# Cross-attention and a mixture-of-experts layer on one core: a fourth joint product, and a new order of the work in a quad

## The chip, the core and the metric

The kernel runs on one core of one Trainium2 chip. The metric is the device time of one execution in microseconds (us), lower is better. A core has five engines that each work through their own list of instructions in order and meet through semaphores: TensorE (PE; its weight loads are shown apart as PEld), VectorE (DVE), ScalarE (ACT), GpSimd (POOL) and SyncE (SP), which here issues all DMAs.

## The reference

For 8 batches of 1024 rows of 1024 float32 numbers:

```
x = x + attention(layernorm(x), ctx, mask)          # 64 context rows a batch, softmax over them
h = layernorm(x)
base = h @ weight.T                                  # 1024 x 1024
probs = softmax(h @ router_w.T)                      # 8 experts; the two best, renormalized
expert_out = sum over experts (w_dense * (h @ lora_A.T)) @ lora_B.T * 2     # rank 16 each
x = x + base + expert_out
```

Everything is computed in float32.

## The kernel before, in words

The 8192 rows are 64 tiles of 128 rows; two tiles (r = 0, 1) form a *pair*, 32 pairs in all, four pairs to a batch. The kernel is software-pipelined over pairs, and the main loop `quad(u)` handles the dense layer of pairs u and v = u+1 while it does the attention and the normalization of later pairs: n = u+2, m = u+3 and f = u+4. The order of instructions on TensorE, VectorE, ScalarE and SyncE is that in which the Python code calls them (a manual schedule), so the order of calls in `quad` is the order on each engine's queue. There are 15 quads (u = 2, 4, ..., 30); `start` and `first_joint` do pairs 0 and 1 and lead in.

**Dense layer.** The base product of a pair is done with seven block products instead of eight (a Strassen-Winograd scheme over two halves of rows, of depth and of columns). Products 1, 6, 7 and the low-rank term 8 of one pair follow each other in one PSUM bank, `chain`; after each, VectorE adds the bank to a quarter of x (`product_add`), and only then may the next product go on in the bank. Product 5 has a bank of its own (`b5`) and is added to two quarters. Products 2, 3 and 4 of two pairs are done *jointly* (`joint`): the same scheme once more, seven blocks of 256 columns instead of eight, in two banks. The sums that they need are made on VectorE (`rt_sums` of a pair, `joint_sums` of two pairs; `quarter_sums` of the weights, once).

**Low rank and router.** `rt_low_rank` multiplies a pair by 136 columns (128 low-rank and 8 router); ScalarE copies the result (`axl`), `rt_top` finds the two best experts on VectorE with one Exp on ScalarE and scales the low-rank numbers; `rt_turn_low_rank` transposes them on TensorE (`trw`), ScalarE copies that (`axwt`), and `lora` adds them to a bank.

**Attention of a pair.** `att_turn` transposes its rows on VectorE from a blocked load (`load_xs`, eight DMAs); `att_scores` (`sct`) multiplies them with the turned context memory (`memT`), ScalarE copies them, `att_sc` transposes them, `att_exp` and `att_divide` do the softmax with row statistics of x, `att_turn_p` transposes the probabilities (`ptp`), ScalarE copies them (`pt`), `att_readout` (`ro`) multiplies them with the memory into four banks, and `att_add` adds these to x. `x_stats` makes the row statistics on ScalarE (two passes with accumulation, then a square root).

**Normalization of a pair.** `norm_stats` makes means and variances on VectorE, `norm` applies them on ScalarE (h), writes h to DRAM and reads it back blocked (`norm_send`), and `rt_turn` transposes it on VectorE into hA and hB.

**Memory of a batch.** Once in four pairs `mask_bias`, `send_mem` (statistics and centring on VectorE, a round trip through DRAM, a scaling pass on ScalarE) and `turn_mem` prepare the next batch's context.

**What sets the order around the change.** Six PSUM banks serve all products, readouts and joints (`bank_of`), one bank the attention scores and probabilities, one the low rank. Six SBUF buffers (`ring`) serve blocked loads, turned rows, h and its reload. Five buffers hold x of pairs, so a load of x for m takes the buffer of pair u-2 and waits until that pair's rows are stored. SyncE issues its DMAs in order, and a DMA waits until the one eight places before it has landed.

Of the kernel before, what the change touches and what calls it, by code (L numbers as in the profile page):

```python
# [24 lines left out]
def kernel(  # L25
# [42 lines left out]
    small = ctx.enter_context(tc.tile_pool(name="small", bufs=2))  # L68
# [118 lines left out]
    def x_stats(u: int):  # L187

        sm = small.tile([P, 2, 1], F32, tag="sm", name=f"sm_{u}")
        nm = small.tile([P, 2, 1], F32, tag="nm", name=f"nm_{u}")  # L190
        ss = small.tile([P, 2, 1], F32, tag="ss", name=f"ss_{u}")
        for r in range(2):
            nc.scalar.activation(  # L193
                junk, xts[u][:, r, :], AF.Identity, accum_out=sm[:, r, :]
            )
        nc.scalar.mul(nm, sm, -1.0 / D)
        for r in range(2):
            nc.scalar.activation(  # L198
                junk, xts[u][:, r, :], AF.Square, bias=nm[:, r, :], accum_out=ss[:, r, :]
            )  # L200
        stds[u] = small.tile([P, 2, 1], F32, tag="std_att", name=f"std_att{u}")
        nc.scalar.activation(stds[u], ss, AF.Sqrt, bias=eps_sb[:, 1:2])

    xmv = {}

    def x_stats_vector(u: int, r: int):
        if r == 0:
            xmv[u] = small.tile([P, 2, 2], F32, tag="mv_att", name=f"mv_att{u}")
# [9 lines left out]
    junk = const.tile([P, D], mybir.dt.bfloat16, name="junk")  # L218

# [7 lines left out]
    def centre_mem(b: int, chunks: bool):  # L227
# [5 lines left out]
        if (b, "mv") not in mcs:  # L233
            mv = small.tile([P, 2], F32, tag="mv_mem", name=f"mv_mem_{b}")
# [16 lines left out]
    def turn_mem_pe(b: int, chunks: bool):  # L251
        mc = centre_mem(b, chunks)
        mt = memp.tile([P, KD, M], F32, tag="memT", name=f"memT_{b}_{chunks}")
# [17 lines left out]
    def turn_mem(b: int):  # L271
        mt = memp.tile([P, KD, M], F32, tag="memT", name=f"memT_{b}_True")
# [27 lines left out]
    def att_scores(u: int):  # L300
# [9 lines left out]
        scs[u] = small.tile([2 * M, P], F32, tag="tp", name=f"scts_{u}")  # L310
# [35 lines left out]
    def att_turn_p(u: int):  # L346
        ptp = ps_at.tile([2 * M, P], F32, tag="at", name=f"ptp_{u}")
        nc.tensor.transpose(ptp, ps.pop(u).rearrange("p j m -> p (j m)"), ident)
        pts[u] = small.tile([2 * M, P], F32, tag="tp", name=f"pt_{u}")
# [64 lines left out]
    has, hbs, axls, axwts, sms = {}, {}, {}, {}, {}  # L414
# [21 lines left out]
    def rt_low_rank(u: int):  # L436

        axls[u] = small.tile([P, 2, ER + E], F32, tag="axl", name=f"axl_{u}", bufs=1)
        pa = ps_rt.tile([P, 2, ER + E], F32, tag="rt", name=f"pa_{u}")
        for r in range(2):  # L440
            for k in range(KD):
                h = (has[u] if k < KH else hbs[u])[:, r, k % KH, :]
                mm(pa[:, r, :], h, art_sb[:, k, :], start=(k == 0), stop=(k == KD - 1))  # L443
        nc.scalar.copy(axls[u], pa)
# [32 lines left out]
    def rt_turn_low_rank(u: int):  # L477
# [4 lines left out]
        axwts[u] = small.tile([ER, 2, P], F32, tag="axwt", name=f"axwt_{u}")  # L482
# [16 lines left out]
    def rt_sums(u: int):  # L499

        outs = [
            sums.tile([P, KH, P], F32, tag=f"s{i}", name=f"s{i}_{u}", bufs=1 if i < 4 else 2)
            for i in range(1, 5)
        ]
        ha, hb = has[u], hbs[u]
        for do in block_sums(outs, ha[:, 0], hb[:, 0], ha[:, 1], hb[:, 1]):
            do()
        sms[u] = outs
# [37 lines left out]
    def block(bank, a, w, start: bool, between=None, after: int = 0):  # L546
        n = a.shape[1]
        for k in range(n):
            mm(bank, a[:, k, :], w[:, k, :], start=(start and k == 0), stop=(k == n - 1),  # L549
               skip_group_check=True)  # L550
            if k == after and between:
                between()
# [3 lines left out]
    def product(u: int, i: int, between=None, after: int = 0):  # L556

        if i == 1:
            pps[u] = bank_of(f"b5_{u}"), bank_of(f"ch_{u}")
# [3 lines left out]
        elif i == 5:  # L563
            block(b5, sms[u][0], t1, True, between, after)
        elif i == 6:
            block(chain, sms[u][1], t2, False, between, after)
        elif i == 7:
            block(chain, sms[u][2], t3, False, between, after)
# [11 lines left out]
    L2 = {2: (0, 0), 3: (0, 1), 4: (1, 0)}  # L580

    def joint_plain(i: int, p: int, between=None, after: int = 0):
# [4 lines left out]
            2: (hbs[p][:, 0], w21), 3: (sms[p][3], w22), 4: (hbs[p][:, 1], t4)  # L587
# [7 lines left out]
    def joint_sums(i: int, u: int):  # L595

        both = i != 3
        outs = [
            sums.tile([P, 2, HK, P], F32, tag=f"q{j}", name=f"q{j}_{i}_{u}")
            for j in range(1, 5)  # L600
        ]
        if both:
            up, lo = hbs[u], hbs[u + 1]
            do = block_sums(
# [378 lines left out]
```

## Time and profile before

| what | value |
|---|---|
| median of 3 runs | 1159.88 us (1159.77 to 1162.51) |
| profiled execution | 1160.02 us, its span 1158.2 us |
| mean granted TensorE clock | 0.995 |
| busy TensorE / VectorE / ScalarE | 1136.2 / 880.7 / 416.4 us |
| one quad in the middle | 69.25 us, or 69.58 us where the memory of a batch is prepared |
| DMA | 175.70 MB, 53.5% of 16 engines' span |

In lines of the profile, L549 is line 549 of the kernel. A group gives line, engine, operation, output tile <- input tiles, sizes and count, then busy time, mean ns of one instruction, and idle time before it with what ended it. A float32 product appears as two records on TensorE. In timelines the first number is the start from the span's beginning and the second the length, both in us; neighbours on TensorE overlap in their drain, so the distance from one start to the next is what a piece of work costs its queue. Where an instruction waited, the wait stands in brackets with its releaser.

### The profile page before, as it was taken

What the parts mean: (1) busy time and instruction counts of PE and PEld (TensorE: products, weight loads), DVE (VectorE), ACT (ScalarE), POOL (GpSimd) and SP (SyncE); (2) the same over time, 40 slices, a digit from 0 to 9 for tenths busy, and PEclk for the clock granted to TensorE, in tenths of its full rate; (3) what the DMA queues carried; (4) which work ended last, traced back from release to release, by engine and by line L of the source; (5) the groups of instructions that cost most, each with busy time, mean ns of one, the idle gap of its engine ahead of it and who ended that gap; (6) DMA issues with size and microseconds to landing.
All of it is one profiled execution on the core that took longest, in us unless ns stands there. A gap on an engine that the chain in (4) does not pass through costs nothing.

```text
span 1158.2 us, 15206 instructions
## 1 busy us (share of the span) xinstructions
PE 1136.2 (98%) x5314; PEld 741.9 (64%) x5314; DVE 880.7 (76%) x2216; ACT 416.4 (36%) x808; POOL 1.0 (0%) x16
## 2 busy tenths in 40 slices
PE   7899999999999999999999999999999999999998
PEld 6455567585665857567585765857567585765746
DVE  5867877887778787787787877788777887777754
ACT  4254333433235342333423234342333433234100
POOL 0000000000000000000000000000000000000000
PEclk8999999999999999999999999999999999999999
DMA  9437655464584635766355674445656374572401
GB/s 238 111 91 200 182 146 189 120 162 148 145 236 116 196 96 146 211 162 204 90 146 162 164 218 117 175 124 165 185 145 202 97 183 137 146 218 73 146 1 72
DMA packets 103549, 175.70 MB, mean 152 GB/s; under 512 B 11376, under 2 KB 75760, under 8 KB 103472
## 3 DMA queue, kind: packets, MB, share of 16 engines
q1 hardware_dynamic: 103472, 174.73, 53.5%
q8 instruction: 41, 0.67, 0.3%
q14 instruction: 36, 0.29, 0.1%
HBM read 107.84 MB, written 66.85 MB: 151 GB/s over the span
## 4 chain that ended last, share of the span: by engine, by line
PE 91%; DVE 5%; DMA 3%; issue 1%; SPq 0%; DVEq 0%
PE ch L549 28%; PE jl L549 13%; PE pa L443 10%; PE ju L549 9%; PE b L549 9%; PE ro L359 5%; PE sct L306 5%; PE jl L543 3%; PE ju L543 3%; PE ch L543 2%; PE j L549 2%; DMA w<-in_w_t_dram 2%; DVE xt L540 1%; DMA xs<-in_x_dram 1%; PE trw L481 1%
## 5 line engine op out<-in xcount | busy, mean ns | idle before, releaser
L549 PE MATMUL ch<-t,s 128*128 128x512 f32 x512 | 242.2, 600 | 3.8 <-DVE xt L540 3.6
L540 DVE TENSOR_TENSOR xt<-ch,xt 128x512 f32<-128x512 f32 x128 | 87.0, 679 | 94.4 <-PE ch L549 57.8
L549 PEld LDWEIGHTS ch<-t,s 128*128 128x128 f32 x512 | 89.8, 190 | 98.1 <-issue 86.9
L382 ACT ACTIVATE std_ffn<-mv_ffn,eps_sb 128x1 f32<-128x1 f32 x64 | 18.9, 296 | 281.0 <-DVE mv_ffn L183 265.9
L549 PE MATMUL ch<-w,hA 128*128 128x512 f32 x256 | 118.3, 605 | 0.1
L549 PE MATMUL b<-w,s 128*128 128x512 f32 x256 | 118.4, 592 | 0.0
L549 PEld LDWEIGHTS ch<-w,hA 128*128 128x128 f32 x256 | 48.0, 192 | 59.6 <-issue 58.4
L630 DVE TENSOR_TENSOR xt<-jl,xt 128x256 f32<-128x256 f32 x135 | 55.5, 411 | 37.3 <-PE jl L549 37.3
L540 DVE TENSOR_TENSOR xt<-ro,xt 128x512 f32<-128x512 f32 x128 | 79.2, 675 | 3.7 <-PE ro L359 3.7
L549 PEld LDWEIGHTS b<-w,s 128*128 128x128 f32 x256 | 46.4, 190 | 55.4 <-issue 54.9
L182 DVE BATCH_NORM_STATS2 st_ffn<-xt 128x6 f32<-128x512 f32 x128 | 80.5, 671 | 0.0
L400 ACT ACTIVATE h<-xt,nmr,rstd_ffn 128x1024 f32<-128x1024 f32 x60 | 71.1, 1232 | 12.3 <-DVE rstd_ffn L389 6.3
L443 PEld LDWEIGHTS pa<-art_sb,hA 128*128 128x128 f32 x512 | 66.3, 190 | 8.4 <-issue 7.4
L89 DVE STREAM_TRANSPOSE xT<-xs 128x1024 f32<-128x1024 f32 x60 | 70.8, 1218 | 0.0
L443 PE MATMUL pa<-art_sb,hA 128*128 128x136 f32 x512 | 69.8, 279 | 0.0
L443 PE MATMUL pa<-art_sb,hB 128*128 128x136 f32 x512 | 69.7, 279 | 0.0
L198 ACT ACTIVATE junk<-xt,nm 128x1024 bf16<-128x1024 f32 x60 | 69.0, 1151 | 2.0
L359 PE MATMUL ro<-mem,pt 64*128 64x512 f32 x256 | 65.4, 630 | 0.4 <-ACT pt L350 0.4
L443 PEld LDWEIGHTS pa<-art_sb,hB 128*128 128x128 f32 x512 | 64.1, 190 | 0.0
L193 ACT ACTIVATE junk<-xt 128x1024 bf16<-128x1024 f32 x60 | 63.6, 1059 | 0.9
L306 PEld LDWEIGHTS sct<-xT,memT_True 128*64 128x64 f32 x960 | 51.8, 137 | 16.6 <-DVE xt L540 10.6
L540 DVE TENSOR_TENSOR xt<-jl,xt 128x512 f32<-128x512 f32 x45 | 31.0, 689 | 41.3 <-PE jl L543 41.3
(151 smaller groups left out, 1767.6 us busy)
## 6 DMA issues: line engine op xcount, KB each, us to landing
out_dram<-xt SPq DMA_DIRECT2D x64, 512.0 KB, 4.4
xs<-in_x_dram SPq DMA_DIRECT2D x240, 128.0 KB, 4.9
xt<-in_x_dram SPq DMA_DIRECT2D x30, 1024.0 KB, 6.7
hd<-h SPq DMA_DIRECT2D x60, 512.0 KB, 2.8
hs<-hd SPq DMA_DIRECT2D x240, 128.0 KB, 3.3
mem<-in_ctx_dram SPq DMA_DIRECT2D x16, 256.0 KB, 6.8
w<-in_w_t_dram SPq DMA_DIRECT2D x16, 256.0 KB, 9.9
xt<-in_x_dram SPq DMA_DIRECT2D x4, 512.0 KB, 6.0
```

The costliest lines, as they stand in the source:

```text
L89: nc.vector.transpose(dst.rearrange("p k (t i) -> p t k i", i=NB), src.rearrange("p t (k i) -> p t k i", i=NB),)
L182: nc.vector.bn_stats(st[:parts, c, :], src[:, ts(c, HB)])
L193: nc.scalar.activation(junk, xts[u][:, r, :], AF.Identity, accum_out=sm[:, r, :])
L198: nc.scalar.activation(junk, xts[u][:, r, :], AF.Square, bias=nm[:, r, :], accum_out=ss[:, r, :])
L306: mm(sct[r * M : (r + 1) * M, :], mt[:, k, :], x_ts[u][r][:, k, :], start=(k == 0), stop=(k == KD - 1),)
L359: mm(ro, pts[u][rows, :], m[rows, ts(c, HB)], start=True, stop=True)
L400: nc.scalar.activation(h, xts[u][:, r, :], AF.Identity, bias=nmr, scale=rstd)
L443: mm(pa[:, r, :], h, art_sb[:, k, :], start=(k == 0), stop=(k == KD - 1))
L540: tt(xc, bank, xc, ALU.add)
L543: mm(bank, axwts[u][:, r, :], lb_sb[:, c0 : c0 + n], start=False, stop=True, skip_group_check=True)
L549: mm(bank, a[:, k, :], w[:, k, :], start=(start and k == 0), stop=(k == n - 1), skip_group_check=True)
L630: tt(xc, src, xc, ALU.add)
```

## The change

- **Product 5** is done jointly for two pairs from quad 2 on, by the function `joint`, with quarters of the weight block t1; it adds no low-rank term, and each add goes to both row tiles of x (the bank read twice, through a broadcast). `rt_sums` keeps its first and fourth sum side by side, so that one `joint_sums` serves products 5 and 3.
- **Joint products** 5, 3, 2, 4 follow each other. Other work is put between their seven blocks by numbered hooks.
- **Readout of a pair** stands right before the scores of the following pair: n before m, m before f. The attention of a pair is half a quad further ahead than before.
- **Low rank** of a pair is split by row tile and stands between products 1, 6 and 7 of the same pair.
- **Statistics** of the normalization go from VectorE to ScalarE (`f_sums`, `f_squares`, `f_std`, `f_rows`); those of the attention are split in three calls.
- **Loads**: the blocked rows of pair u+5 are loaded after the row-0 stores and ahead of the row-1 stores.
- The pool of small tiles has one buffer by default, with two for tiles that are named so.

```diff
-    small = ctx.enter_context(tc.tile_pool(name="small", bufs=2))
+    small = ctx.enter_context(tc.tile_pool(name="small", bufs=1))
...
+    def x_sums(u: int):
...
+        for r in range(2):
+            nc.scalar.activation(
+                nowhere, xts[u][:, r, :], AF.Identity, accum_out=sm[:, r, :]
+            )
+        nc.scalar.mul(nm, sm, -1.0 / D)
+        stds[u] = nm
...
+    def f_std(u: int):
+        nm, ss = fts[u]
+        std = small.tile([P, 2, 1], F32, tag="stdf", name=f"stdf_{u}")
+        nc.scalar.activation(std, ss, AF.Sqrt, bias=eps_sb[:, 0:1], scale=1.0 / D)
+        fts[u] = nm, std
+
+    def f_rows(u: int):
+
+        nm, std = fts.pop(u)
+        rstd = small.tile([P, 2, 1], F32, tag="rstdf", name=f"rstdf_{u}")
+        nc.vector.reciprocal(rstd, std)
+        nmr = small.tile([P, 2, 1], F32, tag="nmrf", name=f"nmrf_{u}")
+        tt(nmr, nm, rstd, ALU.mult)
+        for r in range(2):
+            h = ring.tile([P, D], F32, tag="ring", name=f"h_{u}_{r}")
+            hss.setdefault(u, []).append(h)
+            nc.scalar.activation(
+                h, xts[u][:, r, :], AF.Identity, bias=nmr[:, r, :], scale=rstd[:, r, :]
+            )
+        norm_send(u)
...
+    def rt_low_rank_tile(u: int, r: int):
+        if r == 0:
+            pas[u] = ps_rt.tile([P, 2, ER + E], F32, tag="rt", name=f"pa_{u}")
+        pa = pas[u]
+        for k in range(KD):
+            h = (has[u] if k < KH else hbs[u])[:, r, k % KH, :]
+            mm(pa[:, r, :], h, art_sb[:, k, :], start=(k == 0), stop=(k == KD - 1))
+        if r == 1:
+            axls[u] = small.tile([P, 2, ER + E], F32, tag="axl", name=f"axl_{u}", bufs=1)
+            nc.scalar.copy(axls[u], pas.pop(u))
...
-    def joint(i: int, u: int, early=(), fill=()):
+    def joint(i: int, u: int, hooks):
...
         block(p4, d[:, HK:], q4, True)
-        lora(v, p4, r, c * HB, HH)
-        for do in early[:1]:
-            do()
+        low(v, p4, 0)
+        hook(1)
         block(chain, a[:, :HK], b11, True)
         part(u, 0, chain)
-        for do in early[1:]:
-            do()
+        hook(2)
         block(p2, a[:, HK:], b21, True)
-        lora(u, p2, r, c * HB, HH)
+        low(u, p2, 0)
+        hook(3)
         block(p5, s1, q1, True)
         part(v, 1, p5)
+        hook(4)
         block(chain, s2, q2, False)
         part(u, 1, chain)
-        for do in fill:
-            do()
+        hook(5)
         block(p5, s4, b22, False)
-        lora(u, p5, r, c * HB + HH, HH)
+        low(u, p5, 1)
+        hook(6)
         block(chain, s3, q3, False)
         part(v, 0, chain)
-        add(u, upper, r, c)
+        to_x(u, upper, 0, HB)
+        hook(7)
...
     def first_joint():
...
-        rt_low_rank(2)
         x_stats(4)
         quarter_sums("w22", w22)
         end = joint_plain(4, 0)
+        turn_mem(1)
+        att_turn(4)
+        load_xs(5)
+        end()
+        att_scores(4)
         rt_sums(2)
...
     def quad(u: int):
...
         product(u, 1)
         pending.pop()()
+        product_add(u, 1)
         if more:
             load_xt(m)
         if new_mem:
             load_mem(b)
...
+        rt_low_rank_tile(u, 0)
         rt_turn(v)
+        product(u, 6)
+        if more:
+            att_turn(m)
         product_add(u, 6)
+        if far:
+            load_xs(f)
+            load_xt(f)
+        rt_low_rank_tile(u, 1)
+        product(u, 7)
         rt_top(u)
+        if more:
+            x_sums(m)
+            x_squares(m)
         product_add(u, 7)
+        if more:
+            att_readout(n)
+            att_scores(m)
+            rt_turn_low_rank(u)
+            att_add(n)
         rt_sums(v)
         if u == 2:
+            quarter_sums("w21", w21)
+
+        if more:
+            product(v, 1, {0: lambda: att_sc(m), 2: lambda: product(u, 8)})
+            x_root(m)
             att_rstd(m)
             att_exp(m)
+            product_add(u, 8)
+            product_add(v, 1)
+            if new_mem:
+                mask_bias(b)
+                send_mem(b)
+            f_sums(n)
+            att_divide(m)
+            rt_low_rank_tile(v, 0)
+            product(v, 6, lambda: att_turn_p(m), 1)
+            f_squares(n)
+            f_std(n)
...
+        if far:
+            att_turn(f)
         product_add(v, 6)
+        rt_low_rank_tile(v, 1)
+        product(v, 7)
         rt_top(v)
+        if more:
+            f_rows(n)
+        if new_mem:
+            turn_mem(b)
         product_add(v, 7)
+        one, two = joint_sums(5, u)
+        one()
         if more:
             att_readout(m)
+        if far:
+            att_scores(f)
+        if u == 2:
+            quarter_sums("t4", t4)
+        if more:
+            rt_turn_low_rank(v)
             att_add(m)
+        two()
+
+        def low_v():
+            product(v, 8)
+            product_add(v, 8)
...
+        if far:
+            x_sums(f)
+            x_squares(f)
+            x_root(f)
+            hooks[3] = [lambda: att_sc(f)]
+        end_5 = joint(5, u, hooks)
+
+        hooks = {1: [end_5]}
+        if more:
+            f_sums(m)
+            hooks[5] = [lambda: rt_turn(n)]
+        if far:
+            hooks[2] = [lambda: att_rstd(f), lambda: att_exp(f)]
+        end_3 = joint(3, u, hooks)
+
         one, two = joint_sums(2, u)
         one()
+        hooks = {1: [end_3], 2: [two]}
+        if more:
+            f_squares(m)
+            f_std(m)
+            hooks[5] = [lambda: f_rows(m)]
+        if far:
+            hooks[3] = [lambda: att_divide(f), lambda: att_turn_p(f)]
+        end_2 = joint(2, u, hooks)
+
+        def rows_0():
+            end_2()
             for p in (u, v):
                 store(p, 0)
+            if m + 2 < NP:
+                load_xs(m + 2)
+
+        hooks = {1: [rows_0]}
+        if more:
+            hooks[5] = [lambda: rt_sums(n)]
+        end_4 = joint(4, u, hooks)
```

## The prediction

> **What bounds the kernel now.** I read the page's busy shares and chain first, then equal stretches of the steady middle, then the timelines of single engines in one quad (398 to 467 us).
>
> ```profile
> PE 1136.2 (98%) x5314; PEld 741.9 (64%) x5314; DVE 880.7 (76%) x2216; ACT 416.4 (36%) x808; POOL 1.0 (0%) x16
> PE 91%; DVE 5%; DMA 3%; issue 1%; SPq 0%; DVEq 0%
> ```
>
> ```profile
> 259.23:328.48 69.25, 69.25 (x329) 45.94 (x329) 52.84 (x135) 25.37 (x50) 0.00 (x0) 1.00 0.53 150
> 328.48:398.06 69.58, 69.53 (x330) 45.86 (x329) 56.00 (x143) 26.69 (x52) 0.00 (x0) 1.00 0.61 170
> ```
>
> The second fence has one quad a line: length, then busy time of TensorE, weight load, VectorE, ScalarE; 1.00 is the granted clock. TensorE is busy for the whole quad. So the change can gain only the TensorE work that it removes, and every new TensorE wait adds to the end in full. VectorE (53 of 69 us) is free on average; what counts is whether a given result is there when TensorE asks for it.
>
> **TensorE work removed.** Start-to-start times are the price.
>
> ```profile
> 430.39 2.74 PE L549 MATMUL b<-w,s 128*128 128x512 f32 x6
> 432.97 0.27 PE L348 MATMUL ptp<-ident,s 128*128 128x128 f32 x1
> 433.08 1.02 PE L549 MATMUL b<-w,s 128*128 128x512 f32 x2
> 433.94 1.88 PE L549 MATMUL ch<-t,s 128*128 128x512 f32 x4
> ...
> 444.88 1.03 PE L549 MATMUL jl<-w,q 128*128 128x256 f32 x4
> 445.75 1.03 PE L549 MATMUL ju<-w,q 128*128 128x256 f32 x4
> 446.61 0.59 PE L543 MATMUL ju<-lb_sb,axwt 128*128 128x256 f32 x2
> ```
>
> Product 5 of one pair lasts 433.94 - 430.39 - 0.11 (the transpose inside) = 3.44, two pairs 6.88. Joint, it is seven blocks of 445.75 - 444.88 = 0.865: 6.05. Saved 0.83 a quad. A readout or scores run uses another array shape; the product block after a readout takes 3.63 (421.18 to 424.81) against 3.43 otherwise, so an edge is worth 0.1; adjacent readout and scores save about two: 0.2. Low rank between products costs the same 3.71 in two halves. Together -1.03 x 15 quads = -15.5. In the last quad product 6 waits 1.38 and 0.78 for an add; low rank now stands between: -2.2. Sum -17.7.
>
> **The wait at the probabilities of f (joint 2, hook 3).** The edit moves both turns of n into hook 5 of joint 3 (was one), and puts a softmax division and a TensorE transpose of its result after the second block of joint 2. The same stretch before, on VectorE:
>
> ```profile
> 445.95 0.42 DVE L630 TENSOR_TENSOR xt<-jl,xt 128x256 f32<-128x256 f32 x1 [0.44 <-PE jl L549]
> 446.29 0.70 DVE L89 STREAM_TRANSPOSE hA<-hs 128x512 f32<-128x512 f32 x1
> 446.91 0.67 DVE L89 STREAM_TRANSPOSE hB<-hs 128x512 f32<-128x512 f32 x1
> ...
> 448.45 0.68 DVE L540 TENSOR_TENSOR xt<-ju,xt 128x512 f32<-128x512 f32 x1
> 449.04 0.68 DVE L490 TENSOR_TENSOR q<-hB 128x512 f32<-128x512 f32 x1
> 449.76 0.69 DVE L491 TENSOR_TENSOR q<-q,hB 128x512 f32<-128x512 f32 x1
> ```
>
> Let A be the end of the block "chain, s2" of joint 3 (445.75 above). VectorE then runs in its order: latency 0.20, 256-wide add 0.34, four turns 4 x 0.60, add 0.34, 512-wide add 0.59, sums 0.72 + 0.61, add 0.60, add 0.33, sums 1.20, reciprocal 0.19, division 0.29, 0.07 to TensorE: A + 7.88. TensorE has, up to that transpose, five blocks of 0.865 and four low-rank terms of 0.43: A + 6.04. Nothing can pass the transpose on TensorE's queue: it waits 1.84. This is in quads u = 2 to 26 (13): +23.9. It ends at nothing only if I mis-sized VectorE by 25%; the upper end is 2.3.
>
> **The loads moved ahead of the row-1 stores, and statistics ahead of the score copy.** Loads xs(f+1), eight DMAs, now follow the row-0 stores, so they stand on SP ahead of the row-1 stores and of xt(m).
>
> ```profile
> 399.57 0.33 SPq L662 DMA_DIRECT2D out_dram<-xt  x1
> ...
> 404.07 0.39 SPq L108 DMA_DIRECT2D xt<-in_x_dram  x1
> ```
>
> ```profile
> SPq L108 <- DMA out_dram<-xt: 25.6, 14, 2.8
> ```
>
> xt(m) takes the buffer of pair u-2 and waits for its row-1 store: issued at t = 1.7 (t from the quad's start, 397.90), landed and xt issued at 6.2, landed 6.7 later. Before, nobody wanted it until t = 20.9. Now SP, from h(m) at t = -8.9 (7.6 us of sends and reloads as before), issues the stores at -1.2, eight loads at 0.46, two of which wait for those stores to land (4.4): until 4.05; the store waits until the load two places after them lands (4.9) and goes at 4.55, lands 8.95; xt lands 15.65. On ScalarE sums and squares of m (2 x 1.18 + 0.23 + 2 x 1.27 = 5.14) stand ahead of the score copy (0.27): done at 21.1. TensorE asks for it at 19.6 (products 1, 6, 7: 10.3; low rank 3.7; a 0.43 term; readout and scores 4.1; transposes 0.2; 0.86): waits 1.6. Behind it stand low-rank copies and Exp, which then arrive in time. Bounds: 0 (landings at their shortest) and 2.3 (all bytes in line at the 216 GB/s of the 1 KB reads and about 400 of the stores). I take 1.6, by the median landings, in 13 quads (u = 4 to 28): +20.8.
>
> **New memory in the same chain (6 quads, u = 4 to 24 by 4).** Its bias, statistics and centring (2.9 us on VectorE: 507.66 to 510.56) now stand between the adds of products 8 and 1 and the division of m: that transpose is 0.6 late. ScalarE's scaling of the memory (1.15) waits for it, and the sums of n behind it start 5.1 later than in other quads. From the adds done at t = 23.9 (with no load wait): scaling 26.8 to 28.0, sums 30.6, copy 30.9, squares 33.4, table load and root 35.0, low-rank copy 35.35; top-two on VectorE with its Exp 38.4; reciprocal and product 38.8; memory turned 39.4. The scores of f want that memory at 36.5. Wait 3.0 to 3.1, sum 3.7 x 6 = +22.2. A load wait shifts both sides alike. Bounds 2.5 and 5.
>
> [...] ScalarE's table loads go from 4 to 8 a quad. The row: a load starts at 423.93 and lasts 1.28, the next ACTIVATE starts at 425.23, at once. [...] I take the row.
>
> [...]
>
> ```profile
> 57.36 0.81 PE L256 MATMUL trm_True<-ident,memc_True 64*128 64x64 f32 x8 [3.06 <-DVE memc_True L238]
> 58.11 5.23 PE L549 MATMUL ch<-w,hA 128*128 128x512 f32 x8
> ```
>
> ```profile
> 58.00:62.00 4.00, 4.00 (x8) 1.81 (x7) 2.19 (x2) 0.59 (x1) 0.00 (x0) 0.60 0.61 144
> ```
>
> After a wait of 3.06 and small transposes the granted clock fell to 0.60 and a block of 3.43 took 5.05: +1.6. By that row alone six waits of 3.1 cost +10 more. [...] I take 0 for the six, 1.6 for the wait of 6.0 below, and keep the rest in the range.
>
> **Start and first quads.** Scores of pair 4 now come right after joint_plain(4, 0), at 111.5 (107.15 + 4.3). They need the turned memory, which follows weight quarters on VectorE (111.51 + 2.5), and its reload (109.70 issued, 1.7 + 3.3: 114.5), then two turns (2.36): 117.5. Wait +6.0, clock +1.6. In quad 2 the weight quarters (2.5 each) delay an add and a joint sum: 0.7 + 1.4 = +2.1.
>
> **What costs about nothing.** Row statistics leave VectorE (4 x 1.49 = 6.0 a quad); wider joint sums and two-row adds give back 3.7. ScalarE goes from 26 to some 46 us, still under 70. In joint 5 a 512-wide add comes back to TensorE 0.95 after its block and the bank is wanted 0.865 after: 0.1 a quad, +1.5. Single buffers in the small pool are reused half a quad apart; without that cover the next scores would wait for one softmax.
>
> **Sum.** -17.7 + 23.9 + 20.8 + 22.2 + 9.7 + 1.5 = +60.4 on the span of 1158.2: 1218.6, and with the 1.8 around it 1220.4. The profiled execution (1160.02) stands 0.1 above the median of the runs, so 1220.
>
> **Rivals.** (a) The vector wait alone: loads land early and memory is in time. Then -17.7 + 23.9 + 9.7 + 1.5: 1177. For it: landings as short as 2.6 occur; against: DMA is fully busy in that stretch (shares of 0.9 to 1.1). (b) Faster: the vector stretch before the probabilities' transpose is covered. Its price is 13 times the wait; with the other two hidden, the kernel is faster once that wait is under 0.5, and ends near 1152 at zero. For it: VectorE's busy share falls. Against: fifteen instructions in strict order, each with a row. [...] (d) The edits cancel within 3.5 us (0.3%, about what a measurement of this kernel can tell).
>
> **How the numbers follow.** The full sum 0.62 (own range 1200 to 1237), (a) 0.19, (c) 0.08, (b) 0.08, (d) 0.03. So faster 0.08, same 0.03, slower 0.89. The range 1166 to 1242 leaves out (b), (d) and the far end of (c).
>
> **What would show it.** Joint 5's blocks at 0.865; waits of the transpose ptp on VectorE near 1.8 and of sc on ScalarE's copy near 1.6, once a quad; scores waiting for memT by 3 us in six quads; xt landing after t = 15; TensorE busy time down some 13 while the span grows. The prediction is wrong if quads come in under 69 us, or if ptp starts within 0.3 us of the block before it.

## The result, and the profile after

| | before | changed |
|---|---|---|
| median of 4 runs each, us | 1161.2 | 1235.64 (1234.45 to 1238.28) |
| ratio | | 1.0644, 95% interval 1.0618 to 1.0669 |
| profiled execution's span, us | 1158.2 | 1236.4 |
| mean granted TensorE clock | 0.995 | 0.981 |

The changed kernel is slower by 6.4%. Its page, busy shares and chain:

```profile
PE 1144.7 (93%) x5494; PEld 783.4 (63%) x5494; DVE 863.1 (70%) x2026; ACT 614.1 (50%) x1086; POOL 1.0 (0%) x16
PE 49%; DMA 19%; DVE 18%; ACT 11%; issue 2%; SPq 1%; DVEq 0%; ACTq 0%
```

TensorE was in 91% of the chain and is now in 49%: loads, VectorE and ScalarE set the time in turn. One quad, and one with new memory, as stretches (length, then busy time of TensorE, weight load, VectorE, ScalarE):

```profile
433.17:505.01 71.84, 68.80 (x341) 48.04 (x340) 51.07 (x121) 39.81 (x70) 0.00 (x0) 1.00 0.51 147
505.01:580.23 75.22, 69.06 (x341) 47.96 (x340) 54.32 (x129) 40.85 (x71) 0.00 (x0) 1.00 0.55 153
```

They were 69.25 and 69.58. TensorE's busy time fell only to 68.80; 3.0 us of the first and 6.2 of the second are waits. What TensorE waits for, over the whole run (total, times, longest):

```profile
PE ptp L406 <- DVE s L401: 26.5, 20, 1.7
PE sc L377 <- ACT scts L369: 21.3, 15, 2.8
PE sct L364 <- DVE memT_True L89: 14.6, 6, 2.4
PE sct L364 <- DVE xT L89: 5.9, 2, 5.3
PE ch L620 <- DVE xt L609: 4.6, 11, 0.9
```

The first four are the waits of the prediction: probabilities of f (22 us of the first line; the rest is the probabilities of m, 0.49 in each quad with new memory, and one wait of 1.6 in the lead-in), score copy of m, new memory, scores of pair 4. The fifth, product 7 behind an add that stands behind the turn of m on VectorE, was not in it.

**Probabilities of f.** TensorE, then VectorE in the same quad:

```profile
490.94 0.59 PE L612 MATMUL ju<-lb_sb,axwt 128*128 128x256 f32 x2
493.22 0.30 PE L406 MATMUL ptp<-ident,s 128*128 128x128 f32 x1 [1.69 <-DVE s L401]
```

```profile
485.83 0.70 DVE L89 STREAM_TRANSPOSE hA<-hs 128x512 f32<-128x512 f32 x1
...
491.99 0.68 DVE L559 TENSOR_TENSOR q_j<-hB,hB 128x512 f32<-128x512 f32 x1
492.59 0.16 DVE L400 RECIPROCAL rden<-den 128x2 f32<-128x2 f32 x1
492.78 0.29 DVE L401 TENSOR_TENSOR s<-s,rden 128x128 f32<-128x128 f32 x1
```

The low-rank term costs its queue 0.43, so the transpose could have started at 491.37; it starts at 493.22, 1.85 later. The idle time that the profile prints is 1.69; the other 0.16 is overlap with the matmul before (the term prints 0.59 where its queue pays 0.43), which a start after a wait does not have. So this wait costs its printed length and 0.16. VectorE has no gap in this stretch.

**The load and the score copy.** SyncE's queue, then ScalarE, then TensorE (the quad begins at 433.17):

```profile
433.55 5.03 SPq L83 DMA_DIRECT2D xs<-in_x_dram  x8
438.74 0.93 SPq L749 DMA_DIRECT2D out_dram<-xt  x2
443.65 0.39 SPq L108 DMA_DIRECT2D xt<-in_x_dram  x1
```

```profile
449.10 1.06 ACT L192 ACTIVATE junk<-xt 128x1024 bf16<-128x1024 f32 x1 [2.83 <-DMA xt<-in_x_dram]
...
452.98 1.15 ACT L201 ACTIVATE junk<-xt,nm 128x1024 bf16<-128x1024 f32 x1
...
454.13 0.24 ACT L369 COPY scts<-sct 128x128 f32<-128x128 f32 x1
```

```profile
454.43 0.33 PE L377 MATMUL sc<-ident,scts 128*128 128x128 f32 x1 [1.15 <-ACT scts L369]
```

Eight loads, then the row-1 stores, then x of m, which lands at 449.1, 15.9 us into the quad; over the 13 quads it lands 15.8 to 17.5 us in. The copy of the scores stands behind two passes of sums and two of squares.

**New memory, twice the same.** TensorE in two quads, readout and scores:

```profile
392.82 1.99 PE L417 MATMUL ro<-mem,pt 64*128 64x512 f32 x8
397.24 3.62 PE L364 MATMUL sct<-xT,memT_True 128*64 128x128 f32 x32 [2.43 <-DVE memT_True L89]
...
541.52 1.99 PE L417 MATMUL ro<-mem,pt 64*128 64x512 f32 x8
545.95 1.97 PE L364 MATMUL sct<-xT,memT_True 128*64 128x128 f32 x32 [2.44 <-DVE memT_True L89]
```

The same wait, but behind the first the scores take 3.62 and behind the second 1.97. The four us after each wait (the granted clock is the figure after POOL's busy time):

```profile
397.20:401.20 4.00, 3.96 (x35) 3.70 (x36) 3.96 (x7) 1.93 (x3) 0.00 (x0) 0.57 0.65 258
545.90:549.90 4.00, 3.95 (x43) 3.57 (x44) 3.97 (x7) 3.50 (x7) 0.00 (x0) 1.00 0.66 262
```

The clock was 0.57 in one and 1.00 in the other; the last section shows where the two differ. A quad's length less its printed waits comes to 68.8 to 69.3 in seven of the 13 quads between the readouts of quad 2 and quad 28, and to 70.3 to 70.8 in six: 9.9 us in all are lost to such slow stretches.

**Where the 78.2 us of the span went:**

| term | summed before, us | in the trace, us |
|---|---|---|
| TensorE work and joint 5's stall, last quad's waits | -16.2 | -17.1 (0.94 x 15 as the last experiment shows it undisturbed; waits 3.56 to 0.52) |
| probabilities of f | +23.9 | +24.0 (13 x 1.85) |
| score copy of m | +20.8 | +22.8 (20.7 printed, 13 x 0.16) |
| new memory | +22.2 | +19.0 (6 x 2.51 at the scores, 6 x 0.65 at the probabilities) |
| scores of pair 4, with the clock | +7.6 | +8.8 (5.9 + 0.2, slow 2.7) |
| weight quarters in quad 2 | +2.1 | +1.1 (waits 2.1, less 1.2 that was there before, and restarts) |
| product 7 behind the turn of m | 0 | +4.4 (nine waits of 0.17 to 0.94, and restarts) |
| slow stretches in the 13 quads | 0 | +9.9 |
| lead-in ahead of the first edit | 0 | +4.2 |
| sum | +60.4 (rounded) | +77.1 |

The instructions of TensorE and VectorE are the same up to the low-rank product of the lead-in, which starts at 107.15 before and at 111.31 after. Most of the last term is slow stretches: up to there the clock stood at 0.50 for 17.1 us instead of 10.2, which can cost 3.4 (an estimate: half the difference). But TensorE also waits 0.64 for h at 55.97, in every profile of a kernel with the change and not in that of before, and the readout of pair 3 starts at 102.6 to 105.4 in all of them against 100.8. So part of the term may belong to the change; that stays open. The 1.1 between the sum and 78.2 is assigned to nothing. The profiled execution is also the slowest of its four, 2.6 above their median.

### The profile page after: what moved, and what is told of

The parts are those of the page before. It is cut to its first block, busy times and chain, and to the rows that moved or that the text cites. A ratio compares the mean times of both kernels' runs of the same rounds, so it can differ in the third digit from the quotient of the medians.

```text
span 1236.4 us, 15655 instructions
## 1 busy us (share of the span) xinstructions
PE 1144.7 (93%) x5494; PEld 783.4 (63%) x5494; DVE 863.1 (70%) x2026; ACT 614.1 (50%) x1086; POOL 1.0 (0%) x16
## 4 chain that ended last, share of the span: by engine, by line
PE 49%; DMA 19%; DVE 18%; ACT 11%; issue 2%; SPq 1%; DVEq 0%; ACTq 0%
PE jl L620 13%; PE ch L620 11%; PE ju L620 10%; DMA out_dram<-xt 7%; DMA xt<-in_x_dram 6%; DMA xs<-in_x_dram 3%; PE pa L505 3%; PE sct L364 3%; DVE xt L705 3%; ACT junk L201 3%; ACT junk L192 2%; DVE xt L609 2%; PE ch L612 2%; PE jl L612 2%; PE ju L612 2%
## 5 line engine op out<-in xcount | busy, mean ns | idle before, releaser
L620 PE MATMUL ch<-t,s 128*128 128x512 f32 x512 | 236.1, 600 | 5.0 <-DVE xt L609 4.6
L705 DVE TENSOR_TENSOR xt<-jl,xt 128x256 f32<-128x256 f32 (+1 forms) x240 | 134.1, 569 | 108.9 <-PE jl L620 69.9
L508 ACT COPY axl<-pa 128x272 f32<-128x272 f32 x32 | 12.0, 376 | 269.9 <-PE pa L505 269.9
L620 PE MATMUL ch<-w,hA 128*128 128x512 f32 x256 | 126.6, 620 | 0.2 <-ACT hA L343 0.2
L705 DVE TENSOR_TENSOR xt<-ju,xt 128x256 f32<-128x256 f32 (+1 forms) x120 | 78.3, 652 | 57.8 <-PE ju L620 55.8
L273 ACT ACTIVATE h<-xt,nmrf,rstdf 128x1024 f32<-128x1024 f32 x56 | 66.5, 1234 | 67.8 <-DVE nmrf L269 67.8
L192 ACT ACTIVATE junk<-xt 128x1024 bf16<-128x1024 f32 x60 | 63.4, 1057 | 44.7 <-DMA xt<-in_x_dram 43.7
L364 PEld LDWEIGHTS sct<-xT,memT_True 128*64 128x64 f32 x960 | 57.8, 148 | 43.5 <-DVE memT_True L89 19.6
L364 PE MATMUL sct<-xT,memT_True 128*64 128x128 f32 x960 | 65.9, 294 | 20.5 <-DVE memT_True L89 14.6
L252 ACT ACTIVATE junk<-xt,nmf 128x1024 bf16<-128x1024 f32 x56 | 64.2, 1146 | 1.0
L242 ACT ACTIVATE junk<-xt 128x1024 bf16<-128x1024 f32 x56 | 58.7, 1049 | 1.5 <-DVE xt L609 0.5
## 6 DMA issues: line engine op xcount, KB each, us to landing
w<-in_w_t_dram SPq DMA_DIRECT2D x16, 256.0 KB, 10.2
```

The source lines that it names most:

```text
L192: nc.scalar.activation(nowhere, xts[u][:, r, :], AF.Identity, accum_out=sm[:, r, :])
L252: nc.scalar.activation(nowhere, xts[u][:, r, :], AF.Square, bias=nm[:, r, :], accum_out=ss[:, r, :])
L273: nc.scalar.activation(h, xts[u][:, r, :], AF.Identity, bias=nmr[:, r, :], scale=rstd[:, r, :])
L364: mm(sct[r * M : (r + 1) * M, :], mt[:, k, :], x_ts[u][r][:, k, :], start=(k == 0), stop=(k == KD - 1),)
L705: tt(xc, src, xc, ALU.add)
```

## Experiments

Each kernel is the changed one with the edit shown, unless said otherwise. Differences to the changed kernel are taken between the ratios to the kernel before, times 1161; they are good to about 4 us.

### The division later

```diff
-            hooks[3] = [lambda: att_divide(f), lambda: att_turn_p(f)]
+            hooks[4] = [lambda: att_divide(f)]
+            hooks[6] = [lambda: att_turn_p(f)]
```

> The softmax division of f moves behind the add of the block p5 (hook 4 of joint 2) and the transpose of its result to hook 6; nothing else changes. My theory (separate waits, each with its own cause, which add up): the wait of 1.69 us at this transpose goes in 13 quads and nothing takes its place, since every result that TensorE asks for after it is then on time: -22 us, 1214. The rival (VectorE is 1.7 us behind at this point whatever is asked of it, so the next add that TensorE needs is late by as much): most of the 22 comes back as waits of the blocks of joints 2 and 4 on VectorE's adds, and the time stays above 1228.

1201.17; ratio 1.0355 (1.0336 to 1.0375): 34 us less than the changed kernel. The list of TensorE's waits has

```profile
PE ptp L406 <- DVE s L401: 4.6, 7, 1.6
```

instead of 26.5 in 20: the 13 waits are gone and none took their place; VectorE was late for this one result only. The rival falls. The gain is 12 us more than the 22 expected: in its profile the score copy waits 16.8 instead of 21.3, and two quads instead of six have a slow stretch, some 11 us together.

### The copies between sums and squares

```diff
         rt_top(u)
         if more:
             x_sums(m)
-            x_squares(m)
...
             att_scores(m)
             rt_turn_low_rank(u)
+            x_squares(m)
             att_add(n)
```

> On ScalarE the score copy and the low-rank copy now stand between the sums and the squares of m, so the copy no longer waits for the squares (2.5 us); the loads are where they were. My theory: the wait of the score transpose on ScalarE (20.7 us in 13 quads) goes, and with it the three slow stretches of TensorE behind its longest values (2.1 to 2.8 us), some 5 us; in the six quads with new memory VectorE is no earlier, so the wait at the probabilities of m grows from 0.49 by about 0.9: +5.5. Together -15 to -21, 1215 to 1220. The rival (the late landing of x of m moves the whole softmax of m, and the wait turns up at the next place that needs it, the probabilities of m, in every quad): within 5 us of the changed kernel.

1221.7; ratio 1.0527 (1.0510 to 1.0543): 14 us less, just short of the 15 to 21 expected. The 13 waits of the score transpose are gone (first line; one in the lead-in is left), and with them every slow stretch of the 13 quads. Two other lines grew:

```profile
PE sc L377 <- ACT scts L369: 0.8, 1, 0.8
PE ptp L406 <- DVE s L401: 31.3, 20, 1.7
PE ch L620 <- DVE xt L609: 12.4, 21, 1.0
```

The probabilities of m wait 1.29 instead of 0.49 in the six quads with new memory, as expected (+4.8). The second I had missed: VectorE's add of product 1 of v stands behind the softmax of m, which waits for the root, and product 6 of v now waits 0.52 to 0.98 for that add in all 13 quads. So part of what the copies gain is waited for further on; this much of the rival holds.

### The scaling of the memory later

```diff
         nc.sync.dma_start(out=mcs[b], in_=mc[:M])
-        void_mem(b)
...
         end_3 = joint(3, u, hooks)
+        if new_mem:
+            void_mem(b)
```

> The scaling of the new memory on ScalarE (1.15 us, waiting for the centred memory on VectorE) moves from ahead of the sums of n to behind the Exp of f. My theory (the wait at the scores of f is ScalarE's chain sums, squares, root, held up by this scaling): the sums of n start 4.6 us earlier in six quads, the memory is turned about 542.4 instead of 545.9 in the stretch where TensorE asks for it at 543.4, and the six waits of 2.43 go: -14.6, with up to 5 more from the three slow score runs behind them; 1216 to 1221. The rival (the memory's round trip through DRAM is what is late): the wait stays at 2 us or more and the time is within 4 us of the changed kernel.

1207.98; ratio 1.0401 (1.0385 to 1.0418): 28 us less, where 15 to 20 were expected. VectorE turns the memory, and TensorE asks for it:

```profile
532.92 0.71 DVE L89 STREAM_TRANSPOSE memT_True<-ms 128x512 f32<-128x512 f32 x1
```

```profile
531.92 1.99 PE L416 MATMUL ro<-mem,pt 64*128 64x512 f32 x8
533.84 1.97 PE L363 MATMUL sct<-xT,memT_True 128*64 128x128 f32 x32
```

The readout is followed by the scores without a wait, in all six quads. The round trip through DRAM was in time; one ACTIVATE of 1.15 that waited for VectorE had held up ScalarE's chain. Again the gain exceeds the waits (14.6 and restarts): two slow stretches are left of six, some 6.6 us, and other waits fell by about 2. The last 4 us are within the error.

### The wait filled

```diff
+        if new_mem:
+            fill(5)
         if far:
             att_scores(f)
...
+    def fill(count: int):
+        idle = ps_at.tile([P, HB], F32, tag="at", name="fill")
+        for _ in range(count):
+            mm(idle, ident, w11[:, 0, :], start=True, stop=True)
```

> Ahead of the scores of f in the six quads with new memory TensorE does five matmuls of 512 columns whose result is not used (5 x 0.43 = 2.15 us of the wait of 2.43), so the array works while it waits; the memory comes no earlier. The clock theory (a wait of that length lets the granted clock fall, so that the scores behind it take 3.6 instead of 1.97 in about half of the cases): the scores take 1.97 in all six quads and the mean of the runs falls by some 5 us, 1231. The rival (slow stretches come from something else, or from no event of the program): no change of the time, and slow score runs in some of the six.

1242.22; ratio 1.0711 (1.0687 to 1.0735): 8 us more, where 5 less were expected. I had priced a matmul by one of its two records. It is 0.86, five are 4.3, longer than the wait. In the profile a quad with new memory has 4.55 more work and 2.43 less wait, which would be +12.7 for six; no score run is slow in any of the six. That fits the clock theory, but six cases do not decide it.

### The loads behind the row-1 stores

```diff
                 store(p, 0)
-            if m + 2 < NP:
-                load_xs(m + 2)
...
                 store(p, 1)
+            if m + 2 < NP:
+                load_xs(m + 2)
```

> The loads of the blocked rows go back behind the row-1 stores; all else as in the changed kernel. My theory (the late landing of x of m comes from these eight loads standing ahead of the row-1 stores): x of m lands about 3 us earlier, so the copy no longer waits for the statistics: the wait of the score transpose (20.7 us) and the slow stretches behind it (5) go; the blocked rows land later, and the turns of m on VectorE, with the add behind them, start late: up to 1 us a quad comes back ahead of product 7: 1211 to 1224. The rival (x of m is late because of the traffic itself, whatever stands first): the wait stays above 1 us and the time within 5 us of the changed kernel.

1285.37; ratio 1.1075 (1.1047 to 1.1103): 50 us more than the changed kernel, where 12 to 25 less were expected. The wait of the score transpose is gone from all 13 quads (first line; two in the lead-in are left), so its cause was named rightly. But the next two lines are new:

```profile
PE sc L377 <- ACT scts L369: 0.6, 2, 0.4
DVE xT L89 <- DMA xs<-in_x_dram: 59.5, 26, 4.3
PE ch L620 <- DVE xt L609: 56.8, 15, 5.2
```

The blocked rows land so late that the turns of m wait up to 4.3 on VectorE, and behind them the add that product 7 needs. I had allowed 1 us a quad; it is over 4. The new order needs these loads early. The mend is on ScalarE, as in the copies' experiment. Behind these waits TensorE is slow in every quad (four us from 299.80, clock 0.50):

```profile
299.80:303.80 4.00, 3.95 (x5) 1.85 (x6) 2.29 (x18) 2.25 (x4) 0.00 (x0) 0.50 1.03 199
```

That made this kernel the place to test the clock.

### The same, with TensorE kept at work in the waits

```diff
         rt_low_rank_tile(u, 1)
+        if more:
+            fill(4)
         product(u, 7)
```

> The kernel with the loads behind the row-1 stores, in which product 7 of u waits 3.7 to 5.2 us in 13 quads and TensorE then runs slow (granted clock 0.50 in the four us behind one of these waits; 24.8 us lost in the 13 quads together, by their length less their waits). Now TensorE does four matmuls of 512 columns with an unused result in each of these waits (4 x 0.86 = 3.44 us, less than the shortest), so it stands still for less than 2 us. The clock theory (standing still brings the slow stretch): the slow stretches go, 1260 to 1266. The rival (the slow stretch comes from the transfers or from VectorE's lateness itself, which stay): 1283 to 1287.

1265.82; ratio 1.0897 (1.0873 to 1.0922): 21 us less, although TensorE does 13 x 3.44 = 44.7 us of useless work more, all of it in the waits. TensorE at the same product:

```profile
297.01 3.60 PE L183 MATMUL fill<-w,ident 128*128 128x512 f32 x8
301.07 3.70 PE L626 MATMUL ch<-t,s 128*128 128x512 f32 x8 [0.47 <-DVE xt L615]
```

The block takes 3.70 instead of 6.56. VectorE's add is as late as before: useless work and remaining waits come to 54.0 us in the 13 quads, the waits of the kernel without it to 55.7. So it was the standing still that cost the clock here, and the rival falls. Six of the 13 quads still have a slow stretch: five behind a memory wait of 2.43, which was not filled, and one behind a wait of 2.04 that was left at product 7.

### Scores of pair 4 later

```diff
-        att_scores(4)
         rt_sums(2)
-        end = joint_plain(4, 1, lambda: att_sc(4), 1)
-        att_rstd(4)
-        att_exp(4)
+        end = joint_plain(4, 1)
         quarter_sums("t1", t1)
-        att_divide(4)
...
+        if u == 2:
+            att_scores(4)
         rt_low_rank_tile(u, 0)
         rt_turn(v)
+        if u == 2:
+            att_sc(4)
+            att_rstd(4)
+            att_exp(4)
         product(u, 6)
...
+        if u == 2:
+            att_divide(4)
...
-        product(u, 7)
+        product(u, 7, {1: lambda: att_turn_p(4)} if u == 2 else None)
```

> Only the lead-in and quad 2 change: the scores, softmax and transpose of pair 4 move from between the two plain products 4 to quad 2, each one product later. My theory (the wait of 5.9 us at these scores is a wait for the turned rows of pair 4, which cannot be earlier, and the slow stretch of 2.7 behind it is its consequence): both go, nothing takes their place, -8.6, 1227. The rival (VectorE or ScalarE is late for all of quad 2, so that the wait moves to the probabilities or to the adds of quad 2): above 1232.

1227.96; ratio 1.0565 (1.0538 to 1.0593): 9 us less, as expected. Both waits at these scores and the slow stretch are gone. The readout of pair 4 starts at 137.72 instead of 145.49 in its profile, although products 6 and 7 of quad 2 now wait 1.79 and 1.53 for adds behind the weight quarters. My theory holds within the 4 us, but that nothing takes the place of the wait was wrong.

### Three together

> The division later, the copies between sums and squares and the scaling later, all at once. Alone they gave 34, 14 and 28 us. If these are separate terms: 1236 - 34 - 14 - 28 = 1160, the time of the kernel before. My own sum by waits is less, because the slow stretches of the clock (some 10 us in the changed kernel) were counted in each of the three: waits -22, -20.7 + 5.5 + 7 (waits that the second showed in their place), -14.6, clock -10: 1181. The rival (one wait hides another): above 1190.

1180.18; ratio 1.0157 (1.0136 to 1.0179): 56 us less, where the three alone gave 34 + 14 + 28 = 76. The sum by waits and clock said 1181. Its 13 quads have no wait over 1.3 and no slow stretch. So the waits themselves add up, and what does not is the 10 us of slow stretches, which each of the three had brought down in its own run, and the new waits of product 6 and of the probabilities.

### All mended

On the three: scores of pair 4 as above; the quarters of t1 to where VectorE waits in the lead-in, those of w21 and t4 ahead of `rt_top(v)` in quad 2; and

```diff
+            product_add(u, 8)
             att_rstd(m)
             att_exp(m)
-            product_add(u, 8)
             product_add(v, 1)
-            if new_mem:
-                mask_bias(b)
-                send_mem(b)
             f_sums(n)
             att_divide(m)
+            if new_mem:
+                mask_bias(b)
+                send_mem(b)
...
-            att_turn(m)
-        product_add(u, 6)
+        product_add(u, 6)
+        if more:
+            att_turn(m)
```

> The three together, and four more moves of the same kind: scores of pair 4 in quad 2; the weight quarters t1, w21 and t4 in stretches where VectorE waits; the adds of products 6 and 8 of u ahead of the turn and the softmax of m; the memory's preparation behind the division of m. By the waits that the three together still show (1178.8 in its profile): start -8, quad 2 -2, probabilities of m -7.7, waits of products on adds -9: 1152, so 1150 to 1158 and faster than the kernel before. The rival (VectorE and ScalarE have no room left for this order, so that each move opens a new wait): above 1165.

1164.84 (22 runs); ratio 1.0031 (1.0019 to 1.0043). Neither came true: the expected 1150 to 1158 was too low, and the rival's 1165 was just missed. There are two new waits. The scores of pair 5 in quad 2 wait 3.96 for x of pair 5, with a slow stretch behind. In the six quads with new memory product 7 of v waits 0.96 for an add behind the memory's preparation, and in four of them product 6 of v waits 0.3 as well. But the undisturbed quads now show what the change saves:

```profile
420.49:488.80 68.31, 68.31 (x341) 48.12 (x340) 50.59 (x121) 39.41 (x70) 0.00 (x0) 1.00 0.56 158
```

68.31 against 69.25: 0.94 a quad, all of it TensorE's work.

### Product 5 plain

```diff
-        end_5 = joint(5, u, hooks)
+        product(u, 5, {1: lambda: hook5(hooks, 1), 3: lambda: hook5(hooks, 2)})
+        product_add(u, 5)
+        product(v, 5, {0: lambda: hook5(hooks, 3)})
+        def end_5():
+            product_add(v, 5)
```

> The kernel with all mended, with one part of the change undone: product 5 of the two pairs is done as two plain blocks, with its adds, in the place of the joint one (VectorE still makes the joint sums for it). My theory (in a kernel without other waits TensorE's work is the time): the joint product saves 0.83 a quad less a stall of 0.2, so this run is 9 to 12 us slower than the one with all mended. The rival (the sums and the stalls of the joint product eat its gain): within 3 us of it.

The weight quarters of t1, which only the joint product reads, are not made either.

1170.14; ratio 1.0074 (1.0058 to 1.0090), 5 us slower than all mended: less than expected, and more than the rival's 3. An undisturbed quad is

```profile
981.86:1050.82 68.96, 68.96 (x329) 46.01 (x329) 48.35 (x119) 39.46 (x70) 0.00 (x0) 1.00 0.54 151
```

so the joint product is worth 0.65 a quad (0.83 less a stall of 0.2, as expected here), some 10 us in 15. Part of it is given back in waits that are longer in the joint version: 3.96 instead of 2.23 for pair 5 in quad 2, 1.6 instead of 0.52 behind the readout of pair 31 (last quad and the joints before it), and 3.2 instead of 1.5 at the score transposes in between. Together that is 1.7 + 1.1 + 1.7 of the 10. Why these waits are longer there was not tried.

### The wait put back

All mended, with hook 3 of joint 2 as in the changed kernel.

> The kernel with all mended, with the division of f and the transpose of its result back at hook 3 of joint 2. Alone, moving them out had given 34 us where the wait is 22. My theory (12 of these were other waits and slow stretches of the clock, which happened to fall in the changed kernel and need a longer wait than 1.69): here the move costs 22 to 25 us. The rival (a wait of 1.69 us costs more than its length, by a restart or by the clock): 30 us or more.

1191.32; ratio 1.0267 (1.0248 to 1.0285): 27 us slower than all mended (24 to 31), between the two expectations. Its profile shows 13 of these waits of 1.69 and one in the lead-in:

```profile
PE ptp L405 <- DVE s L400: 23.5, 14, 1.7
```

With the restarts the 13 make 24.0, and none has a slow stretch behind it. So the wait costs little more than its length; the interval does not exclude a few us beyond it.

### Two more moves

On all mended; `mem_stats` is the part of `send_mem` that makes the statistics, and stands behind `rt_sums(v)`.

```diff
+        if new_mem:
+            mask_bias(b)
+            mem_stats(b)
...
+        end()
+        store(0, 1)
         load_xs(5)
```

> On the kernel with all mended: the row-1 store of pair 0 goes ahead of the loads of the blocked rows of pair 5 (so that x of pair 5 lands in time in quad 2), and the bias and statistics of a new memory are made before the softmax of m, where VectorE waits 2 us for the root. My theory: the wait of 3.96 in quad 2 with the slow stretch of 1.6 behind it goes, and of the six waits of 0.96 to 1.27 on VectorE's adds at least 0.8 each: -8 to -10.5 on 1164.8, so 1154 to 1157, faster than the kernel before by 0.4 to 0.6%. The rival (VectorE's work is only moved, so that the probabilities of m wait by as much, and the load of pair 5 is late from traffic): 1162 or more, no faster than before.

1157.92; ratio 0.9964 (0.9948 to 0.9980): 8 us less than all mended, just short of what was expected, and a little faster than the kernel before, by 0.2 to 0.5%. An undisturbed quad and one with new memory:

```profile
537.82:606.13 68.31, 68.31 (x341) 48.13 (x340) 50.57 (x121) 39.49 (x70) 0.00 (x0) 1.00 0.51 151
606.13:675.69 69.56, 68.75 (x341) 48.05 (x340) 53.69 (x129) 40.53 (x71) 0.00 (x0) 1.00 0.61 171
```

With its waits mended the change is worth some 4 us of the 14 (0.94 x 15) by which TensorE's work fell; its score transposes alone still wait 6.6 in the run.

## Why the prediction was right or wrong

The sign and the mechanism were right; the time came out 15.6 above the 1220 and inside the range, near the upper end of the likeliest case's own. One sign failed: TensorE's busy time was to fall by some 13 and rose by 8.5 (1136.2 to 1144.7), because matmuls in the slow stretches (scores of 3.62 instead of 1.97) and restarts behind waits (up to 0.16 each) print as busy time.

**TensorE's work: right in sum.** -0.93 a quad was summed (0.83 + 0.2 less 0.1 of stall); 0.94 is seen where nothing disturbs it. The parts were each a little off: the joint product gave 0.65 instead of 0.73, the rest of the change 0.29 instead of 0.2. In a quad of the changed kernel that has no slow stretch the busy time fell by only half of the sum.

**The probabilities of f: right**, 1.85 against 1.84. Fifteen VectorE instructions, each by its own row, in strict order, give a wait to a hundredth. The wait went away when two calls moved to later hooks, so its cause was the place of the transpose and not VectorE's amount of work.

**The score copy: right in cause; that the mean fits is in part luck.** 1.6 is printed on average (1.75 with the restart) against 1.6, though the prediction's own times, 21.1 less 19.6, give 1.5. Its landing of x of m, 15.65 against a measured 15.8 to 17.5, is made of two misses that cancel: SyncE issued the load at 10.4 to 11.2 instead of 8.95, and eleven of the 13 loads took 5.3 to 5.9 instead of 6.7. The median wait is 1.4; three landings at 16.7 to 17.5 brought waits of 2.1 to 2.8 and lift the mean (two others as late brought 1.5 and 1.6, since product 7 had already waited there). The step left out what is late next on the other side: the blocked rows of m, which make product 7 wait by 0.2 to 0.9 (+4.4).

**New memory: right in cause, 3 us too high.** The scores wait 2.51 from start to start instead of 3.0 to 3.1 (the prediction's own times, 39.4 less 36.5, give 2.9): ScalarE's chain was summed 0.6 too long. The table load there took its own 1.28 and no more: it starts 0.02 after the instruction before it, and the next ACTIVATE starts 0.01 after its end:

```profile
539.77 0.18 ACT L252 ACTIVATION_READ_ACCUMULATOR junk<-xt,nmf 128x1 f32 x1
539.97 1.28 ACT L260 ACT_TABLE_LOAD   x1
541.26 0.30 ACT L260 ACTIVATE stdf<-ssf,eps_sb 128x2 f32<-128x2 f32 x1
```

So the row that the prediction took held.

**The clock: the step that failed.** The prediction read one row (0.60 after a wait of 3.06) and put 0 for the six memory waits. It did not put the question to the score copies at all, since their mean is 1.6. No run shows the 0: in the trace three memory waits of 2.43 and three score waits of 2.1 to 2.8 have a slow stretch behind them: 9.9 us. The row was the better guide. In it TensorE stood still for 2.96 of the 3.41 us from 54.40 to 57.81 of the profile before, and the clock is 0.50 in the next 3.41; in the changed kernel 2.10 to 2.82 us of standing still in one stretch of 3.41 came ahead of the six slow ones (last section). And a mean wait of 1.6 hides the few that are long enough.

**Start: right in kind.** 6.1 against 6.0 for the wait; the slow stretch behind it 2.7 against 1.6.

**The rivals.** (a), loads and memory in time, is ruled out by their waits. (b), faster, did not happen (and its end near 1152 is 1153.5 by its own terms); moving the probabilities alone left the kernel 3.6% slower than before, and only the last kernel, with all mends and two more moves, was faster, by 0.2 to 0.5%. (c), waits longer than summed, came in part: slow stretches took 9.9 us in the 13 quads, but the scores of a new memory waited 2.51 instead of 3.0 to 3.1. (d), edits that cancel, is ruled out by the 6.4%.

## What to carry to other kernels

Where one engine is busy all the time, price a new order by the results that it will ask for: for each, sum the other engine's queue up to it, instruction by instruction; a mean share of free time says nothing. A move that brings a wait is mended by moving the consumer by a few blocks rather than by undoing the move: undoing one of two moves that lean on each other cost 50 us. And look at the longest waits of a kind, not at their mean, where the clock falls behind a wait, as it did here behind score waits of 2.1 to 2.8 whose mean is 1.6.

## What the runs showed of the hardware

**Waits of 1.81 us and more brought the slow clock in 38 of 58 quads, shorter ones in none of 124.** Over the profiles of both kernels and of all experiments, each of the 13 quads between the readouts of quads 2 and 28 was put by its longest TensorE wait, and called slow where its length less its waits (and less the inserted matmuls) is over 1 us above that of undisturbed quads:

| longest wait in the quad, us | quads | slow |
|---|---|---|
| under 1.75 | 124 | 0 |
| 1.81 to 1.93 | 5 | 1 |
| 2.04 to 2.4 | 6 | 6 |
| 2.43, ahead of the scores of a new memory | 28 | 13 |
| 2.5 to 3.3 | 5 | 4 |
| over 3.3 | 14 | 14 |

A slow quad lost 1.2 to 3.2 us, and 4.4 in the one quad with three slow stretches.

**Of equal waits some brought it and some did not.** In all 14 profiles the granted clock is either 1.00 or 0.50, and within a profile its changes (5 before, 23 in the changed kernel) lie a multiple of 3.413 us apart, to within 3 ns. At 0.50 a 128x512 record of a matmul costs 0.85 from start to start instead of 0.43 (medians in the changed kernel, 9 and 736 records), so 3.41 us of it can cost 1.7 (an estimate: half of them). I divided each profile from 140 us on into stretches of 3.41 us, counted from such a change. Of the stretches at full clock in which TensorE stood still for less than 1.8 us, none was followed by a slow one (0 of 4218; in the profiles before and of the changed kernel alone, 0 of 601); from 1.8 to 2.0 us, one of 12 (0 of 2); from 2.0 us on, all (38 of 38; 6 of 6). In the lead-in of the changed kernel, however, 1.81 and 1.82 us were each followed by a slow one. The two equal memory waits of the changed kernel differ in this, here with their stretches (the first number behind the comma is TensorE's busy time):

```profile
393.84:397.25 3.41, 0.98 (x8) 0.15 (x4) 2.85 (x16) 1.55 (x3) 0.00 (x0) 1.00 0.00 0
397.25:400.66 3.41, 3.41 (x32) 3.27 (x32) 3.38 (x6) 1.61 (x2) 0.00 (x0) 0.50 0.61 243
```

```profile
540.61:544.02 3.41, 2.90 (x11) 0.84 (x9) 1.68 (x15) 2.70 (x5) 0.00 (x0) 1.00 0.00 0
544.02:547.43 3.41, 1.48 (x28) 1.48 (x29) 3.26 (x11) 2.23 (x2) 0.00 (x0) 1.00 0.04 17
547.43:550.85 3.42, 3.42 (x23) 2.56 (x20) 3.42 (x7) 2.92 (x7) 0.00 (x0) 1.00 0.87 301
```

The first wait lies in one stretch, 2.43 of 3.41, and the next is slow. The second is divided at 544.02; the larger part is 1.93, and the clock stays. The other four memory waits of the changed kernel agree: 2.38 and 2.43 in one stretch (from 690.79 and 840.98) have a slow one behind, 1.85 and 1.53 (from 243.65 and 991.17) have none. Over all profiles waits of 2.43 brought a slow stretch in 13 of 28 cases.

**Work without use kept the clock up.** Useless matmuls in waits of 3.7 to 5.2 us took 21 us off a run (ratio 1.1075 to 1.0897), and six of 13 quads were slow instead of 13.

**A wait cost up to 0.16 more than it printed** (1.85 against 1.69 at the probabilities, 2.51 against 2.44 at the scores of a new memory): the overlap with the matmuls before, which print 0.59 and 1.99 where their queue pays 0.43 and 1.92.
